# Graph encoder on one core: a separate buffer for the last keys' adjacency, a new order of VectorE's work at part ends, and three late projections emptied by ScalarE

## The chip, the core and the metric

The kernel runs on one core of a Trainium2 chip. The core has five engines, each with an instruction list of its own that it runs strictly in order: TensorE (PE; its weight loads are shown as PEld), VectorE (DVE), ScalarE (ACT), GpSimd (POOL) and SyncE (SP). Here POOL and SP do little but issue DMA transfers. Engines wait for each other through semaphores. Matrix products go into PSUM, which the kernel divides into eight banks of 128 partitions by 512 fp32 numbers; everything else lies in SBUF or in DRAM. The metric is the device time of one execution in microseconds (us).

## The reference

Four graph layers run on the same 2708 nodes of 512 features. The change touches the first part of the first layer, called the encoder here:

```python
Xh = X.reshape(n, H, D).transpose(1, 0, 2)            # H = 4 heads, D = 128
Xw = jnp.einsum('hnd,hde->hne', Xh, W)
f1 = jnp.einsum('hnd,hd->hn', Xw, V[:, 0, :, 0])
f2 = jnp.einsum('hnd,hd->hn', Xw, V[:, 1, :, 0])
sig = jax.nn.sigmoid(f1[:, :, None] + f2[:, None, :])
local_att = _masked_softmax(local_pattern[None] * sig, lmask)
...
Xa = jnp.einsum('hij,hjd->hid', att, Xw)
...
Xn = _batchnorm(Xc, enc_bn_gamma, enc_bn_beta)
emb = _mlp_block(Xn, enc_mlp_W, ...)
```

So for every head there is a 2708 x 2708 table: a sigmoid of a sum of one number per row and one per column, times the 0/1 adjacency, a softmax over the connected nodes, and a product with the projected features. Both masks are the same adjacency here, so one table serves both. The decoder, two more attention layers and a mean layer follow; the change leaves them alone.

## The kernel before

**Tiling.** The table is worked on transposed, keys on partitions. The 2708 keys are 22 blocks (`NT`): 21 of 128 and a last one of 20, "the last keys". The columns (the nodes that receive) are two halves of 1354 (`HW`). The four heads are taken two at a time (`HP`). A *part* is one half with one pair of heads, in the order (half 0, heads 0 and 1), (half 0, heads 2 and 3), (half 1, heads 0 and 1), (half 1, heads 2 and 3). A part has 22 *steps*, one for each key block, 88 steps in all. The last keys come at place 11 of a part; their 20 rows are spread over four groups of partitions, so that their tile is only 384 columns wide (`FEW`).

**One step.** ScalarE forms the sigmoid as a tanh, one 128x1354 instruction for each head (L383). VectorE forms the softmax argument for both heads at once, 128x2708 (L378): tanh plus a constant, times the masked adjacency. ScalarE takes the exponential of it (L515). PE multiplies it with the projected values: for each head, 11 matmuls for 11 blocks of nodes (L548, two records each in the trace). A value block has 129 columns, the last of them ones, so the row sums of the softmax come out beside the product. Three node blocks share a PSUM bank; a head fills four banks (`po`), two heads all eight. They accumulate over the 22 steps of the part.

**The adjacency.** A step's adjacency tile `a` comes on SP's queue (L480) into one of four buffers (677 KB a load). In the first pair of heads of each half it comes raw and VectorE makes the mask from it in two instructions (L443 compares with zero, L444 adds a large negative number), and POOL stores the masked tile in DRAM (L448) for the second pair of heads, which loads it back. For the last keys the four buffers serve as well: small strip loads on SP (L430, L432) fill one of them. Five blocks of the second half are fetched and masked ahead, during the second part (`fetch_early`).

**Order.** A framework puts the instructions of each engine in order when the program is built; the engine then runs that list as it is. `tc.issue_after(x)`, here `behind(x)`, forces an instruction behind another one. Buffers of a pool are reused in turn: an instruction that writes a reused buffer waits until all readers of the earlier content are through, DMA stores among them. The encoder's loop (L560 to L605) works on step *k*: it opens the tanhs of step *k*, issues the exponential of *k*-1, the argument of *k* (`form`), and PE's products of step *k*-2 (`FRONT` = 2), then the mask of step *k*+2.

**Start.** `project` computes the projected values on PE block by block (`values_of`): a 128x512 copy out of PSUM (L317), by ScalarE or VectorE, and a halving of f2 by VectorE (L321, 128x4). The first 17 blocks are done at once. The other five are left for `rest`, which is called after the argument of step 1 and is pinned behind it. There ScalarE copies two of the five, VectorE three; two chunks of f1 follow, and the two small instructions `bm1` and `less` (L343, L344) end it. Then the first mask of the loop runs.

**Part ends.** When PE has finished the last step of a part, `keep` (L759) empties the eight banks: for each head a memset of a column of `rc` (L769) and for each of its groups the largest of sum and a tiny number (L781), the reciprocal (L782), and the product of the values with it (L783, 128x384 for a full bank). `keep` is called behind the newest argument. Then `turn` transposes the rows back on PE (L802), three banks' worth for a head, all in banks of the second head; VectorE or ScalarE copies each to `ft` (L823). In the same bank as a head's third transposed piece lies the transposed `rc` (L810), which VectorE copies to `sm` (L812) and POOL stores to `rs_d` in two DMAs (L814, L818). Statistics of `ft` follow (L825). At part ends `pending` is 2 for a step and 1 for the next, and the exponential of step *k*-1 is then issued behind ScalarE's copies of the second head. The products of later steps into the second head's banks wait for these copies. The last of the four parts has no step behind it: its turns are interleaved with weight transposes (`seam`).

**Pools.** The wide tiles `t`, `rows` among them, have five buffers; `a` has four; `sm` has the default of its pool, two.

Of the kernel before, what the change touches and what calls it, by code (L numbers as in the profile page):

```python
# [8 lines left out]
F32 = mybir.dt.float32  # L9
# [3 lines left out]
AF = mybir.ActivationFunctionType  # L13
ALU = mybir.AluOpType
# [3 lines left out]
P = 128  # L18
# [3 lines left out]
TINY = 1e-30  # L22
# [7 lines left out]
def gnn_stack_kernel(  # L30
# [158 lines left out]
    with ExitStack() as l0:  # L189
# [45 lines left out]
        def project(att, psum):  # L235
# [66 lines left out]

            def values_of(jt, scalar):
                j0, n = BLOCKS[jt]
                pxw = psum.tile([P, H // HP, BANK], F32, tag=f"po{jt % HB}", name="pxw")
                pv = pxw[:, :, : HP * (P + 2)].rearrange("p a (k e) -> p a k e", k=HP)
                for h in range(H):
                    nc.tensor.matmul(
                        pv[:n, h // HP, h % HP, :],
                        xT_sb[:, h, j0 : j0 + n],  # L310
                        w0x[:, h, :],
                        start=True,
                        stop=True,
                    )

                copy = nc.scalar.copy if scalar else nc.vector.tensor_copy
                copy(  # L317
                    xw[:n, jt, :, :P].rearrange("p (a k) d -> p a k d", a=H // HP, k=HP),
                    pv[:n, :, :, :P],
                )  # L320
                nc.vector.tensor_scalar(  # L321
                    f2h[:n, jt, :].rearrange("p (a k) -> p a k", k=HP),
                    pv[:n, :, :, P + 1],
                    0.5,
                    None,
                    ALU.mult,
                )
            AT_ONCE = NT - 5
# [3 lines left out]
            def rest(step):  # L332

                with tc.issue_after(step.ins):
                    for jt in range(AT_ONCE, NT):
                        values_of(jt, jt < AT_ONCE + 2)
# [7 lines left out]
                    return nc.vector.tensor_scalar(  # L344
                        less, prm_sb[:, MB_ENC, :], 1.0, None, ALU.subtract
                    )

# [47 lines left out]
        def encoder_pass(values, att, banks, finish, f1b, blocks, spread, rest):  # L395

            FRONT, LEAD = 2, 2
            tanh, args, exps, tiles, loads, fetched, brought = ([] for _ in range(7))
# [65 lines left out]
            def bring(k):  # L464
# [6 lines left out]
                if k < len(blocks):  # L471
                    a = blocks[k]
                else:
                    a = att.tile([P, HW], F32, tag="a", name="a", bufs=4)
                    if n < P:
                        load_strips(a, src, hf)
                    else:
                        with behind(*[spread] if k < len(blocks) + 2 else []):
                            loads.append(
                                nc.sync.dma_start(a[:n, :w], src[j0 : j0 + n, h0 : h0 + w])  # L480
                            )
# [45 lines left out]
            def form(k, *more):  # L527

                *_, rows, width = rows_of(k)
                t, a = tiles[k]  # L530
                with behind(*args[-1:], *more):
                    args.append(arguments(t[:rows], a, rows, width))

# [26 lines left out]
            for k in range(len(STEPS) + FRONT):  # L560
# [4 lines left out]
                if pending != 1 and 0 < k <= len(STEPS):  # L565
                    exponentials(k - 1)
                if inside and not pending:
                    form(k)
                    if k == 1:
                        args.append(rest(args[1]))  # L570
                        po = banks()
                if k >= FRONT:
                    part, place = STEPS[k - FRONT]
# [162 lines left out]
        with (  # L736
# [20 lines left out]
            def keep(hf, p, po, later):  # L757
# [9 lines left out]
                for k in range(HP):  # L767
                    rc = att.tile([P, NB], F32, tag="rc", name="rc", bufs=4)
                    nc.vector.memset(rc[:, NB - 1 :], 1.0)  # L769
                    rows = all_rows[:, k]  # L770
                    groups = []
                    for b in range(HB + 1):
                        own = list(range(b * PER, min(NB, (b + 1) * PER)))
                        whole = [r for r in own if NODES[hf][r][1] == P]
                        groups += [(b, g) for g in (whole, [r for r in own if r not in whole]) if g]
                    for b, g in groups:
                        m = NODES[hf][g[0]][1]
                        src = po[k][b][:m, g[0] % PER * DR : (g[-1] % PER + 1) * DR]
                        src = src.rearrange("p (r e) -> p r e", e=DR)
                        own = rc[:m, g[0] : g[-1] + 1]  # L780
                        nc.vector.tensor_scalar(own, src[:, :, P], TINY, None, ALU.max)  # L781
                        nc.vector.reciprocal(own, own)  # L782
                        nc.vector.tensor_tensor(  # L783
                            rows[:m, g[0] : g[-1] + 1, :],
                            src[:, :, :P],
                            own.unsqueeze(2).to_broadcast([m, len(g), P]),
                            ALU.mult,
                        )
# [1488 lines left out]
```

## Time and profile before

| | |
|---|---|
| median of three runs | 3121.74 us (3119.06 to 3122.14) |
| the profiled execution, its own time | 3120.7 us |
| its span in the profile | 3118.8 us |
| encoder, first mask of the loop to PE's last product | 41.66 to 487.05 us |
| argument L378, in the encoder | x88, mean 2882 ns |
| tanh L383, in the encoder | x167 full-size, mean 1411 ns |
| exponential L515 | x88, mean 2377 ns |
| mask, L443 and L444, full-size | x37 each, mean 835 and 1510 ns |
| product by the reciprocal L783 | x40, mean 444 ns |
| copies of `ft` L823: ScalarE, VectorE | x15, mean 540 ns; x9, mean 613 ns |
| `sm` copy L812 | x8, mean 269 ns |

How to read the lines that follow. The page gives the busy time of an engine, its share of the span and the number of its instructions. A window line gives, for one stretch of time, its length, and the busy time of PE, PEld, DVE, ACT and POOL with the number of instructions, then the clock granted to PE as a share of full speed, the share of time that the DMA engines were busy, and GB/s. A wait line names an engine, the tile and source line that waited, what released it, then the total in us, how many times, and the longest. A timeline line gives start, duration, engine, source line, operation, out <- in with shapes; a wait that ended there stands in brackets. A DMA line gives size and us from issue to landing. Durations overlap a little at their ends: an instruction of 2.96 us on VectorE can be followed by the next start after 2.89 us.

### The profile page before, as it was taken

The page shows a single profiled execution, that of the slowest core. Times are in us where ns is not written, and L with a number is a line of the kernel's source. Part 1 is how long each engine was busy: PE and PEld are TensorE (multiplying, and loading weights), DVE is VectorE, ACT ScalarE, POOL GpSimd, SP SyncE. Part 2 cuts the span into 40 slices and gives each one's busy share as a digit, 9 for nine tenths or more (in the row PEclk, how much of TensorE's full clock was granted, in tenths as well). Part 3 has the DMA queues.
Part 4 walks back from the last instruction along what each step waited for, and adds up shares of the span by engine and source line. Part 5 has one row for each costly group of instructions (what it writes and reads, how often), then busy time and mean ns, then how long its engine had stood idle before and what let it go on. Part 6 is the DMA issues. An engine that isn't in the chain of part 4 may idle for free.

```text
span 3118.8 us, 39610 instructions
## 1 busy us (share of the span) xinstructions
PE 3070.6 (98%) x15144; PEld 2336.9 (75%) x15144; DVE 2025.3 (65%) x3804; ACT 1353.1 (43%) x1655; POOL 175.2 (6%) x301
## 2 busy tenths in 40 slices
PE   8999999999999999999999999999999999999999
PEld 7999996544444447875588887787778888888886
DVE  7988966785885783452366668677555555555565
ACT  7999998587767350001133334435211111111111
POOL 1111100000000000000111101000010000000000
PEclk9999999999999999999999999999999999999999
DMA  8987964266445315530254445566331111111110
GB/s 277 333 313 251 321 235 144 79 232 221 161 173 192 108 42 158 144 97 31 67 166 133 136 138 165 164 177 184 108 95 36 50 51 51 51 51 50 50 52 29
DMA packets 207228, 430.10 MB, mean 138 GB/s; under 512 B 22218, under 2 KB 137598, under 8 KB 201294
## 3 DMA queue, kind: packets, MB, share of 16 engines
q1 hardware_dynamic: 182774, 326.20, 34.0%
q0 software_dynamic: 24256, 101.35, 8.9%
q8 instruction: 119, 1.95, 0.3%
q14 instruction: 71, 0.58, 0.1%
q10 hardware_dynamic: 8, 0.02, 0.0%
HBM read 330.07 MB, written 95.87 MB: 137 GB/s over the span
## 4 chain that ended last, share of the span: by engine, by line
PE 79%; ACT 8%; DVE 8%; issue 3%; DMA 1%; SPq 0%; DVEq 0%; ACTq 0%; POOLq 0%
PE po L1728 21%; PE ps_s L1523 18%; PE po L650 9%; PE ps_nb L1326 7%; PE ps_wide L1376 5%; PE po L548 4%; ACT t L383 4%; ACT t L515 3%; DVE t L378 2%; PE ps_v L131 2%; PE ps_sup L1934 2%; PE ps_hid L131 2%; PE ps_dec L1093 2%; PE ps_mlp L964 1%; DVE a L444 1%
## 5 line engine op out<-in xcount | busy, mean ns | idle before, releaser
L378 DVE SCALAR_TENSOR_TENSOR t<-t,a 128x2708 f32<-128x2708 f32 (+1 forms) x152 | 443.8, 2922 | 166.1 <-ACT t L383 165.8
L548 PE MATMUL po<-xw,t 128*128 128x129 f32 (+2 forms) x3872 | 428.2, 277 | 11.8 <-DVE rc L781 4.9
L548 PEld LDWEIGHTS po<-xw,t 128*128 128x128 f32 (+2 forms) x3872 | 422.8, 189 | 16.4 <-issue 7.9
L383 ACT ACTIVATE t<-f1b,f2h 128x1354 f32<-128x1354 f32 x296 | 404.4, 1412 | 34.2 <-PE po L650 34.2
L1523 PE MATMUL ps_s<-q,hT 128*128 128x256 f32 (+1 forms) x1848 | 405.5, 372 | 0.0
L1728 PE MATMUL po<-sup,e 128*128 128x256 f32 (+1 forms) x1512 | 398.2, 384 | 5.6 <-DVE c L1809 2.8
L650 PE MATMUL po<-t,emb 128*128 128x452 f32 (+3 forms) x1056 | 399.1, 547 | 4.3 <-ACT t L635 4.2
L1523 PEld LDWEIGHTS ps_s<-q,hT 128*128 128x128 f32 x1848 | 339.5, 190 | 49.5 <-issue 5.1
L650 PEld LDWEIGHTS po<-t,emb 128*128 128x128 f32 (+1 forms) x1056 | 194.2, 191 | 202.1 <-issue 189.2
L1728 PEld LDWEIGHTS po<-sup,e 128*128 128x128 f32 (+1 forms) x1512 | 264.7, 185 | 59.6 <-issue 19.8
L1728 PE MATMUL po<-held,T 128*128 128x256 f32 x1200 | 293.8, 380 | 0.0
L1728 PEld LDWEIGHTS po<-held,T 128*128 128x128 f32 x1200 | 227.0, 190 | 31.1 <-issue 0.9
L2129 DVE SCALAR_TENSOR_TENSOR e<-a_cols,ps_s 128x512 f32<-128x512 f32 (+1 forms) x121 | 79.6, 658 | 233.8 <-PE ps_s L1523 229.9
L1523 PE MATMUL ps_s<-hT 128*128 128x256 f32 (+2 forms) x968 | 213.8, 372 | 0.8 <-ACT sup L1941 0.7
L515 ACT ACTIVATE t<-t 128x2708 f32<-128x2708 f32 x88 | 209.2, 2377 | 8.8 <-DVE t L378 8.1
L1523 PEld LDWEIGHTS ps_s<-hT 128*128 128x128 f32 x968 | 175.1, 190 | 29.1 <-issue 3.9
L1326 PE MATMUL ps_nb<-hid_hi,at 128*128 128x512 f32 x484 | 185.6, 390 | 0.4 <-DVE at L1318 0.4
L635 ACT ACTIVATE t<-t 128x2708 f32<-128x2708 f32 x64 | 157.3, 2458 | 60.4 <-DVE t L378 60.2
L1326 PE MATMUL ps_nb<-hid_lo,at 128*128 128x512 f32 x462 | 180.0, 390 | 0.0
L2031 ACT ACTIVATE a_score<-a_score,neg_big 128x512 f32<-128x512 f32 (+3 forms) x131 | 88.4, 683 | 196.0 <-DMA a_score<-in_adjT_dram 98.9
L2121 ACT ACTIVATE q<-ps_wide,uq 128x256 f32<-128x256 f32 (+1 forms) x44 | 20.5, 465 | 335.7 <-PE ps_wide L1376 335.7
L1633 ACT ACTIVATE e<-e 128x512 f32<-128x512 f32 (+1 forms) x187 | 113.8, 615 | 118.2 <-DVE e L1632 117.9
(276 smaller groups left out, 3995.4 us busy)
## 6 DMA issues: line engine op xcount, KB each, us to landing
a<-adj_d SPq DMA_DIRECT2D x113, 677.0 KB
a_cols<-in_adjT_dram SPq DMA_DIRECT2D x200, 256.0 KB
kept<-t POOLq DMA_DIRECT2D x20, 1354.0 KB, 8.4
t<-kept SPq DMA_DIRECT2D x20, 1354.0 KB
raw<-in_adjT_dram SPq DMA_DIRECT2D x105, 256.0 KB
a<-in_adjT_dram SPq DMA_DIRECT2D x37, 677.0 KB
adj_d<-a POOLq DMA_DIRECT2D x37, 677.0 KB, 6.2
a_score<-in_adjT_dram SPq DMA_DIRECT2D x55, 256.0 KB
```

The source lines that it names most:

```text
L131: nc.tensor.matmul(ps[:n], xt[:, c, :n], w[:, c, :], start=(c == 0), stop=(c == C - 1))
L378: return nc.vector.scalar_tensor_tensor(t, t, GUARD, ab, ALU.add, ALU.mult)
L383: done = nc.scalar.activation(t[:, k, :], f1b[k][:n, :w], AF.Tanh, bias=f2h[:n, jt, h : h + 1], scale=0.5,)
L515: nc.scalar.activation(t, t, AF.Exp, scale=0.5)
L548: nc.tensor.matmul(po[k][b][:m, s * DR : (s + 1) * DR], t[own : own + n, k, i0 : i0 + m], values[own : own + n, jt, HP * p + k, :], start= ...
L635: nc.scalar.activation(t, t, AF.Exp, scale=0.5)
L650: nc.tensor.matmul(po[HB * k + q][:, :qw], values[r : r + n, jt, h * P : (h + 1) * P], t[r : r + n, k, q0 : q0 + qw], start=(place == 0), ...
L1326: nc.tensor.matmul(pos[it][:n], at, half[:, jt, :], start=(jt == 0 and k == 0), stop=(jt == NT - 1),)
L1376: nc.tensor.matmul(ps[:, :width], w(c, o), xt(c), start=(c == 0), stop=(c == C - 1),)
L1523: nc.tensor.matmul(ps[:, jb, i:w], keys[:, c, j : j + P], st["q"][:, c, i:], start=(c == 0), stop=(c == C - 1),)
L1633: return nc.scalar.activation(e, e, AF.Exp)
L1728: nc.tensor.matmul(po[bank][rows, half, :], lhsT, rhs, start=(k == 0 and half == 0) if first is None else first, stop=last, skip_group_che ...
```

## The change

There are three edits, all in the encoder.

*Late projections.* `rest` lets ScalarE copy three of the five late value blocks instead of two. For these three, ScalarE also does the halving of f2, as an activation `Copy` with scale 0.5. `rest` returns two instructions, VectorE's last one and ScalarE's last halving, and the exponential of step 0 is issued behind the latter.

*Last keys' buffer.* The masked or raw adjacency of the last keys gets a buffer of its own, `a_few` of 128x384 numbers, one buffer. It is loaded when the tile of place 4 of a part is brought, behind that tile's load, and taken at place 11. The four `a` buffers serve the 21 full blocks alone.

*Part ends.* In the step that ends a part, the argument is no longer formed ahead of `keep`. Instead `keep` gets it as a function: head 0's banks are emptied behind the argument before, each instruction of the head chained by `behind_this`; then the argument is issued behind head 0's last product; then head 1's banks behind that argument. In the last part, where no argument is left, the function hands its input back. The copies `sm` get one buffer instead of two.

```diff
@@ -300,6 +300,8 @@
                 load_columns(NCH - 1)
                 nc.sync.dma_start(prm_sb, prm)
 
+            AT_ONCE, taken = NT - 5, []
+
             def values_of(jt, scalar):
                 j0, n = BLOCKS[jt]
                 pxw = psum.tile([P, H // HP, BANK], F32, tag=f"po{jt % HB}", name="pxw")
@@ -318,14 +320,13 @@
                     xw[:n, jt, :, :P].rearrange("p (a k) d -> p a k d", a=H // HP, k=HP),
                     pv[:n, :, :, :P],
                 )
-                nc.vector.tensor_scalar(
-                    f2h[:n, jt, :].rearrange("p (a k) -> p a k", k=HP),
-                    pv[:n, :, :, P + 1],
-                    0.5,
-                    None,
-                    ALU.mult,
-                )
-            AT_ONCE = NT - 5
+                half = f2h[:n, jt, :].rearrange("p (a k) -> p a k", k=HP)
+                if scalar and jt >= AT_ONCE:
+                    taken.append(
+                        nc.scalar.activation(half, pv[:n, :, :, P + 1], AF.Copy, scale=0.5)
+                    )
+                else:
+                    nc.vector.tensor_scalar(half, pv[:n, :, :, P + 1], 0.5, None, ALU.mult)
             for jt in range(AT_ONCE):
                 values_of(jt, jt < 2 * NT // 3)
 
@@ -333,7 +334,7 @@
 
                 with tc.issue_after(step.ins):
                     for jt in range(AT_ONCE, NT):
-                        values_of(jt, jt < AT_ONCE + 2)
+                        values_of(jt, jt < AT_ONCE + 3)
                     h0, w = HSPAN[1]
                     for q, (q0, _) in enumerate(HCH[1]):
                         f1_rows(HB + q, later_rows[:, q0:], q == 0)
@@ -341,9 +342,10 @@
                     copies(xw[:, NT - 1].rearrange("p h e -> p (h e)"))
                     copies(f2h[:, NT - 1, :])
                     nc.vector.tensor_scalar(bm1, prm_sb[:, MB_DEC, :], 1.0, None, ALU.subtract)
-                    return nc.vector.tensor_scalar(
+                    last = nc.vector.tensor_scalar(
                         less, prm_sb[:, MB_ENC, :], 1.0, None, ALU.subtract
                     )
+                return last, taken[-1]
 
             return f1b, blocks, spread, rest
 
@@ -395,7 +397,7 @@
         def encoder_pass(values, att, banks, finish, f1b, blocks, spread, rest):
 
             FRONT, LEAD = 2, 2
-            tanh, args, exps, tiles, loads, fetched, brought = ([] for _ in range(7))
+            tanh, args, exps, tiles, loads, fetched, brought, few = ([] for _ in range(8))
             state = {"f1b": f1b}
 
             def rows_of(k):
@@ -470,15 +472,18 @@
                 src = adjT if prepare else adj_d
                 if k < len(blocks):
                     a = blocks[k]
+                elif n < P:
+                    a = few.pop()
                 else:
                     a = att.tile([P, HW], F32, tag="a", name="a", bufs=4)
-                    if n < P:
-                        load_strips(a, src, hf)
-                    else:
-                        with behind(*[spread] if k < len(blocks) + 2 else []):
-                            loads.append(
-                                nc.sync.dma_start(a[:n, :w], src[j0 : j0 + n, h0 : h0 + w])
-                            )
+                    with behind(*[spread] if k < len(blocks) + 2 else []):
+                        loads.append(
+                            nc.sync.dma_start(a[:n, :w], src[j0 : j0 + n, h0 : h0 + w])
+                        )
+                if STEPS[k][1] == 4:
+                    few.append(att.tile([P, FEW], F32, tag="a_few", name="a_few", bufs=1))
+                    with behind(loads[-1]):
+                        load_strips(few[0], src, hf)
                 last_load[:] = loads[-1:]
                 if prepare:
                     mask_block(a, hf, jt, rows, width, *args[-1:])
@@ -530,6 +535,7 @@
                 t, a = tiles[k]
                 with behind(*args[-1:], *more):
                     args.append(arguments(t[:rows], a, rows, width))
+                return args[-1]
 
             def node_sums(k, part, place, t):
 
@@ -562,15 +568,19 @@
                 copies_done = []
                 if inside:
                     open_step(k)
-                if pending != 1 and 0 < k <= len(STEPS):
-                    exponentials(k - 1)
-                if inside and not pending:
+                part, place = STEPS[max(0, k - FRONT)]
+                ends = k >= FRONT and place == NT - 1
+                if pending != 1 and k > 1:
+                    if k <= len(STEPS):
+                        exponentials(k - 1)
+                if inside and not pending and not ends:
                     form(k)
-                    if k == 1:
-                        args.append(rest(args[1]))
-                        po = banks()
+                if k == 1:
+                    done, scalar_done = rest(args[1])
+                    args.append(done)
+                    po = banks()
+                    exponentials(0, scalar_done)
                 if k >= FRONT:
-                    part, place = STEPS[k - FRONT]
                     t, _ = tiles[k - FRONT]
                     if place > 3 and later and part[1] > 0:
                         with behind(args[-1]):
@@ -585,9 +595,10 @@
                         for work in waiting:
                             work()
                         waiting = []
-                    if place == NT - 1:
-                        with behind(args[-1]):
-                            turns = finish(*part, po, later)
+                    if ends:
+                        turns = finish(
+                            *part, po, later, args[-1], lambda done: form(k, done) if inside else done
+                        )
                 if pending == 1:
                     exponentials(k - 1, *copies_done)
                 if inside and pending:
@@ -754,7 +765,7 @@
             mlp_w, last_po, last_later, last_turn = [], [], [], []
             ft = feat_tile("ft")
 
-            def keep(hf, p, po, later):
+            def keep(hf, p, po, later, behind_this, argument):
                 h0, w = HSPAN[hf]
                 if hf == 1 and p == 0:
                     with behind(*last_load):
@@ -766,27 +777,30 @@
                 all_rows = wide_tile(att, "rows").rearrange("p (k r d) -> p k r d", k=HP, d=P)
                 for k in range(HP):
                     rc = att.tile([P, NB], F32, tag="rc", name="rc", bufs=4)
-                    nc.vector.memset(rc[:, NB - 1 :], 1.0)
-                    rows = all_rows[:, k]
-                    groups = []
-                    for b in range(HB + 1):
-                        own = list(range(b * PER, min(NB, (b + 1) * PER)))
-                        whole = [r for r in own if NODES[hf][r][1] == P]
-                        groups += [(b, g) for g in (whole, [r for r in own if r not in whole]) if g]
...
+                    with behind(behind_this):
+                        nc.vector.memset(rc[:, NB - 1 :], 1.0)
+                        rows = all_rows[:, k]
+                        groups = []
+                        for b in range(HB + 1):
+                            own = list(range(b * PER, min(NB, (b + 1) * PER)))
+                            whole = [r for r in own if NODES[hf][r][1] == P]
+                            groups += [(b, g) for g in (whole, [r for r in own if r not in whole]) if g]
+                        for b, g in groups:
...
+                            behind_this = nc.vector.tensor_tensor(
+                                rows[:m, g[0] : g[-1] + 1, :],
+                                src[:, :, :P],
+                                own.unsqueeze(2).to_broadcast([m, len(g), P]),
+                                ALU.mult,
+                            )
                     kept.append((rows, rc))
+                    if k == 0:
+                        behind_this = argument(behind_this)
 
                 final = hf == NHALF - 1 and p + 1 == H // HP
 
@@ -808,7 +822,7 @@
                     cw = min(w, c0 + BANK) - c0
                     if b + 1 == TURNS:
                         done = nc.tensor.transpose(bank[:NB, BANK - P :], rc, ident)
-                        sm = att.tile([NB, P], F32, tag="sm", name="sm")
+                        sm = att.tile([NB, P], F32, tag="sm", name="sm", bufs=1)
                         nc.vector.tensor_copy(sm, bank[:NB, BANK - P :])
                         full = (NB - 1) * P
                         nc.gpsimd.dma_start(
```

More of the change, by code (lines that the diff above doesn't have):

```diff
@@ L776, in keep @@
[L776 to L788, printed above, removed]
+                    with behind(behind_this):
[7 more added lines that the diff above has]
+                        for b, g in groups:
+                            m = NODES[hf][g[0]][1]
+                            src = po[k][b][:m, g[0] % PER * DR : (g[-1] % PER + 1) * DR]
+                            src = src.rearrange("p (r e) -> p r e", e=DR)
+                            own = rc[:m, g[0] : g[-1] + 1]
+                            nc.vector.tensor_scalar(own, src[:, :, P], TINY, None, ALU.max)
+                            nc.vector.reciprocal(own, own)
+                            behind_this = nc.vector.tensor_tensor(
[4 more added lines that the diff above has]
+                            )
```

## The prediction

> **What bounds the kernel now.** I read the page's busy shares first, then busy time by stage, then the waits of each engine inside the encoder, then the timeline of one part end and of the late projections. The change touches the encoder alone (about 30 to 495 us of the 3118.8 us span).
>
> ```profile
> PE 3070.6 (98%) x15144; PEld 2336.9 (75%) x15144; DVE 2025.3 (65%) x3804; ACT 1353.1 (43%) x1655; POOL 175.2 (6%) x301
> ```
>
> The average names TensorE; by stage it is different. Busy time of PE, PEld, DVE and ACT in the four parts:
>
> ```profile
> 41.66:149.00 107.34, 102.97 (x929) 101.71 (x930) 104.27 (x63) 99.91 (x62) 23.48 (x37) 0.98 0.85 298
> 149.00:260.00 111.00, 109.24 (x1002) 108.04 (x1001) 89.63 (x79) 108.56 (x71) 11.88 (x22) 1.00 0.87 318
> 260.00:374.00 114.00, 111.40 (x1003) 110.11 (x1002) 101.39 (x86) 110.27 (x73) 15.86 (x29) 0.99 0.82 291
> 374.00:487.00 113.00, 110.96 (x1018) 110.00 (x1018) 81.24 (x103) 104.46 (x68) 8.17 (x15) 1.00 0.67 214
> ```
>
> In the first part VectorE sets the pace: mask (0.79 and 1.59 us from start to next start) and argument (2.89) make 5.27 us a step. In the other three ScalarE does: two tanhs (2.63) and one exponential (2.35) make 4.98 us. PE is nearly tied: 88 matmul records took 9.85 us at 87.31, 0.112 each, so a step's 44 take 4.93. PE trails: the last exponential runs from 477.77 to 480.23, PE ends at 487.05, 1.9 us more than one step's 4.93.
>
> Where these engines waited (total us, times, longest):
>
> ```profile
> DVE z L443 <- DMA a<-in_adjT_dram: 1.7, 1, 1.7
> ...
> PE po L548 <- DVE rc L781: 4.9, 3, 2.1
> ...
> ACT ft L823 <- PE po L802: 7.0, 5, 1.9
> ...
> ACT ft L823 <- DVE sm L812: 1.8, 2, 1.2
> ```
>
> The second and third line are what the change goes for. The fourth is the one to watch: ScalarE's last copy of a head, out of the bank that also holds the row sums, starts only after VectorE's `sm` copy of those sums. The first part end shows it:
>
> ```profile
> 158.18 2.72 ACT L383 ACTIVATE t<-f1b,f2h 128x1354 f32<-128x1354 f32 x2
> ...
> 160.36 0.27 DVE L812 COPY sm<-po 11x128 f32<-11x128 f32 x1
> ...
> 161.23 2.96 DVE L378 SCALAR_TENSOR_TENSOR t<-t,a 128x2708 f32<-128x2708 f32 x1
> ...
> 164.11 0.27 DVE L812 COPY sm<-po 11x128 f32<-11x128 f32 x1
> ...
> 164.31 2.96 DVE L378 SCALAR_TENSOR_TENSOR t<-t,a 128x2708 f32<-128x2708 f32 x1
> 164.42 0.43 ACT L823 COPY ft<-po 128x330 f32<-128x330 f32 x1 [0.58 <-DVE sm L812]
> ...
> 164.75 2.46 ACT L515 ACTIVATE t<-t 128x2708 f32<-128x2708 f32 x1
> ```
>
> One argument (161.23) stands between the two `sm` copies; the second argument (164.31) comes after both, and the next exponential starts at 164.75.
>
> **The change, part by part.**
>
> *Late projections (about -1.1).* VectorE's stretch behind the second argument runs from 37.91 to the first mask at 41.66, 3.75 us:
>
> ```profile
> 37.91 0.15 DVE L321 TENSOR_SCALAR f2h<-pxw 128x4 f32<-128x4 f32 x1
> 37.98 0.68 DVE L317 COPY xw<-pxw 128x512 f32<-128x512 f32 x1
> 38.57 0.22 DVE L321 TENSOR_SCALAR f2h<-pxw 128x4 f32<-128x4 f32 x2
> ```
>
> One 512-column copy (0.6 to the next start), three halvings (0.07 each) and a 0.24 us wait for PE go: 1.05 us. VectorE is the bound here, so it counts. ScalarE gains one copy (0.50) and three small activations, which the trace does not have in this shape; the nearest row is a 128x4 activation, 0.20 us. They stand ahead of the first exponential, which started at 35.13 and now starts about 36.2. Its cover is VectorE's stretch: the next argument, at 44.92, needs a tanh pair that then ends about 41.3. Bounds -0.8 (the wait returns elsewhere) to -1.3.
>
> *The last keys' own buffer (about -1.7).* The mask at 94.95 waited 1.7 us for a load issued at 87.46, when the store of its buffer's earlier tile had landed. With the last keys out of the four buffers, that load takes the buffer released one 5.27 us step earlier, which is more than the wait. Four small and three smaller strip loads move up on SP, past one 677 KB load there; that load's tile is needed some 10 us later. Bounds: 0, if the full DMA engines (share 0.99 to 1.0 at 85 to 100) only make another load late, and -1.7.
>
> *Banks ahead of the argument.* VectorE empties head 0's four banks as they fill, then forms the argument, then empties head 1. PE no longer waits for `rc` (4.9 us, three times), and ScalarE is not held up by the later argument itself: at the first end the argument would end near 155.8, and ScalarE is busy with tanhs until 155.83. But `sm` now has one buffer instead of two, and in the built program the second `sm` copy has moved: at the first and third end behind both arguments, at the second behind a mask's first half, an argument and a mask's second half. It also waits for the first head's two row-sum stores. Queued behind it: ScalarE's third copy, the exponential behind that copy, and six of PE's matmuls into that bank. Laying rows end to end:
>
> First end: PE's last step (ends 153.6, 4.93 long) fills head 0's first bank at 149.6. Emptying head 0 alone 3.3 (the final turn's: 483.01 to 486.3) gives 152.9; argument 2.89, 155.8; head 1 with three copies and `sm` 4.4 (the 5.25 of 155.98 to 161.23 less head 0's remnants), 160.2; two arguments 2.89 + 2.96, 166.1; `sm` 0.3, copy 0.36: exponential at 166.75 against 164.75, **+2.0**. The stores are no later: they landed at 165.6 and 165.8.
>
> Second end: start 260.0; head 0 3.3, argument 2.89, head 1 2.9, mask 0.8 + 1.6, `sm` and last rows 0.5, argument 2.89, mask 0.79, argument 2.96, mask 1.56, `sm` 0.3, copy 0.36: 280.8. Some 0.4 of the head's short instructions overlap, 280.4 against 277.8, **+2.6** (2.0 to 3.2).
>
> Third end: start 372.9, by the same terms VectorE reaches `sm` at 389.4 and the exponential starts at 390.0 against 388.22, +1.8. But here the stores were slow:
>
> ```profile
> kept<-t POOLq DMA_DIRECT2D x1, 1354.0 KB, 10.2
> ...
> rs_d<-sm POOLq DMA_DIRECT2D x1, 5.0 KB, 7.8
> ```
>
> The row-sum stores queue on POOL behind a kept tile. Issued at 383.3 and 383.8 and landing 7.7 later, 391.5, they put the exponential at 392.2, +4.0; landing when they did before, 392.9, +5.3. I take **+4.0**, between 1.8 and 5.3, by the row of the same two stores.
>
> A page puts such a store lower: the Trainium skill, DMA: Bandwidth & Descriptors, "Anatomy of one DMA", fits about 2.0 us plus bytes over 436 GB/s for one DMA alone. By it the third end would cost 1.8 and the sum be 2.2 less; the rows, 3.4 to 7.8 at the inner ends, decide.
>
> *Final turn (+0.4).* The `argument` call does nothing here; head 1 is emptied strictly after head 0, where the rows of 486.1 to 487.0 show them interleaved: 0.4. `sm` came 2.80 after `sm` and its stores, issued 491.68 and 492.19, took 1.6: no wait. If they took 4, as elsewhere, +2.4.
>
> PE idles longer at the ends, and its clock shows what that does:
>
> ```profile
> 100.00:105.00 5.00, 2.15 (x10) 2.15 (x11) 5.00 (x4) 4.66 (x3) 0.03 (x1) 0.74 1.03 411
> ```
>
> After 3.9 us idle the granted clock was 0.74, then 0.92 for 5 us each: 1.7 us of PE time. The last keys' step takes PE 1.42 us where ScalarE needs 3.4, so PE makes up 2.0 in each part, and I cost it at nothing; without that cover, 1.7 an end. The Trainium skill, TensorE: Matmul & The Clock Gate, "HAM oscillation", warns of PE gaps above about 3.4 us; taken at its halved rate the price would be as much again, 3.4 an end, under the same cover.
>
> **Sum.** -1.05 - 1.7 + 2.0 + 2.6 + 4.0 + 0.4 = **+6.2 us**. Behind the encoder nothing changes. The profiled execution took 3120.7 (span 3118.8 and 1.9 around it), 1.0 below the median; 3126.9 against it, 3127.9 against the median. I forecast **3128**.
>
> **Rivals.** *Stores land early* (2 in 10): `sm` is bound by VectorE alone at all ends: +4.0, 3125.7. For it: the first two ends. Against: the 7.8. *Stores bind everywhere, the mask still waits* (2 in 10): -1.05 + 2.8 + 2.6 + 5.3 + 2.4 = +12, 3133.8. For it: stores issued sooner sit behind the same kept tile, and DMA is full there. *Faster, since PE and not ScalarE sets the end* (0.7 in 10): the bound is PE's list, late exponentials fall into PE's 1.9 us of trail, and 4.9 of `rc` waits go: -1.05 - 1.7 - 4.9 = -7.7, 3114.0. It decides only while exponentials are late by less than 1.9; my first end alone uses that up. *The buffer brings no earlier load*: +7.9, within the main case.
>
> **How the numbers follow.** Main case 5.3 in 10, from +4 to +9, about 3 above and 2.3 below the bound. Against the median, 0.2% (6.2 us, about what a measurement of this kernel can tell from no change) is 3128.0, so the forecast stands on the bound. Slower: 3 + 2 = 5 in 10; same 2.3 + 2 + 0.2 = 4.5; faster 0.5. Range: low end +1, all gains whole and the ends at their low bounds (-1.3 - 1.7 + 1.4 + 2.0 + 1.8 + 0 = +2.2) less 1.2 for the spread of the runs, 3122.7; high end the second rival, 3133.8.
>
> **What would show it.** Right: the first mask near 40.6, no DMA wait of a mask in the first part, `rc` gone from PE's waits; ScalarE's waits for `sm` grown from 1.8 to some 12 to 16 us, 4 to 7 at each inner end, with two arguments between the `sm` copies. Wrong: a short wait of that copy, exponentials on time after the ends, or PE idle for `rc` still.

## The result and the profile after

The changed kernel took 3126.3 us in the median of 12 runs (3122.04 to 3130.19), the kernel before 3119.5 in 12 runs. The ratio is 1.0019, 95% interval 1.0011 to 1.0027: slower by about 6 us. The profiled execution took 3126.66, with a span of 3124.6 against 3118.8.

Every one of the 88 exponentials has a start time in ScalarE's timeline, before and after, so the change can be read as a ladder: how much earlier or later the same exponential starts. It is flat within each part and steps at the places that the edits touch.

| exponential of step | before | after | difference | step of the ladder |
|---|---|---|---|---|
| 4 (behind the late projections) | 58.47 | 57.56 | -0.91 | -0.91 |
| 12 (behind the last keys of part 1) | 100.34 | 97.76 | -2.58 | -1.67 |
| 22 (ahead of the first end) | 150.85 | 148.27 | -2.58 | 0 |
| 24 (behind it) | 164.75 | 166.83 | +2.08 | **+4.66** |
| 44, 46 (around the second end) | 261.13, 277.82 | 263.23, 281.86 | +2.10, +4.04 | **+1.94** |
| 66, 68 (around the third end) | 374.20, 388.22 | 378.24, 393.84 | +4.04, +5.62 | **+1.58** |
| 87 (the last) | 477.77 | 483.40 | +5.63 | 0 |

Behind the encoder another 0.2 is added: the first matmul into `ps_m` starts at 500.51 instead of 494.70, +5.81, which is the whole of the span's difference.

The timelines of the changed kernel where the two gains come from. ScalarE's halving of f2 (L326) is new, and the first mask starts at 40.74 instead of 41.66; the mask that had waited 1.7 us for its load starts at 92.37 with no wait in brackets:

```profile
37.45 0.18 ACT L326 ACTIVATE f2h<-pxw 128x4 f32<-128x4 f32 x1
37.52 2.46 ACT L520 ACTIVATE t<-t 128x2708 f32<-128x2708 f32 x1
...
40.74 0.85 DVE L445 TENSOR_SCALAR z<-a 128x1354 bf16<-128x1354 f32 x1
...
92.37 0.87 DVE L445 TENSOR_SCALAR z<-a 128x1354 bf16<-128x1354 f32 x1
```

What the engines of the changed kernel wait for in the encoder (total us, times, longest):

```profile
DVE sm L826 <- DMA rs_d<-sm: 2.9, 1, 2.9
...
ACT ft L837 <- DVE sm L826: 15.9, 3, 6.5
...
PE po L554 <- ACT ft L837: 7.5, 3, 3.5
```

The 4.9 us for which PE's products waited for `rc` (L793 now) are gone, as the change intends. In their place PE waits 7.5 for ScalarE's copies where it had waited 0.9, and ScalarE waits 15.9 for `sm` where it had waited 1.8. The first part end shows both causes:

```profile
157.46 5.84 DVE L380 SCALAR_TENSOR_TENSOR t<-t,a 128x2708 f32<-128x2708 f32 x2
...
158.94 1.07 ACT L837 COPY ft<-po 128x512 f32<-128x512 f32 x2 [0.62 <-PE po L816]
...
166.19 0.28 DVE L826 COPY sm<-po 11x128 f32<-11x128 f32 x1 [2.88 <-DMA rs_d<-sm]
166.50 0.44 ACT L837 COPY ft<-po 128x330 f32<-128x330 f32 x1 [6.49 <-DVE sm L826]
...
166.83 2.46 ACT L520 ACTIVATE t<-t 128x2708 f32<-128x2708 f32 x1
```

Two arguments (157.46, x2) now stand ahead of the second `sm` copy, where one did. When they are done, at 163.3, VectorE waits another 2.88 us until the first head's row sums have left the one `sm` buffer. ScalarE has copied the rest of the head by 160.0 and stands idle for 6.49 us.

### The profile page after: what moved, and what is told of

It reads as the page before. It is cut to its first block, busy times and chain, and to the rows that moved or that the text cites. A ratio compares the mean times of both kernels' runs of the same rounds, so it can differ in the third digit from the quotient of the medians.

```text
span 3124.6 us, 39587 instructions
## 1 busy us (share of the span) xinstructions
PE 3074.1 (98%) x15144; PEld 2335.7 (75%) x15144; DVE 2026.0 (65%) x3800; ACT 1354.1 (43%) x1659; POOL 176.3 (6%) x301
## 4 chain that ended last, share of the span: by engine, by line
PE 81%; DVE 7%; ACT 6%; issue 3%; DMA 2%; POOL 0%; SPq 0%; DVEq 0%; POOLq 0%; ACTq 0%
PE po L1742 22%; PE ps_s L1537 19%; PE po L661 9%; PE ps_nb L1340 7%; PE po L554 5%; PE ps_wide L1390 5%; ACT t L385 3%; PE ps_sup L1948 2%; PE ps_v L131 2%; PE ps_hid L131 2%; DVE t L380 2%; ACT t L520 2%; PE ps_dec L1107 2%; PE ps_mlp L978 1%; PE ps_e L1670 1%
## 5 line engine op out<-in xcount | busy, mean ns | idle before, releaser
L380 DVE SCALAR_TENSOR_TENSOR t<-t,a 128x2708 f32<-128x2708 f32 x148 | 439.8, 2975 | 169.3 <-ACT t L385 169.1
```

Of the source, the lines that this page charges most:

```text
L380: return nc.vector.scalar_tensor_tensor(t, t, GUARD, ab, ALU.add, ALU.mult)
```

## The experiments

Theory A: the time is lost to the single `sm` buffer, in two ways: the copy stands one argument later on VectorE's list, and it waits for the first head's stores. Theory B: it is lost to emptying head 0 ahead of the argument, since the argument and all behind it come later. The last columns of this table are the steps of the ladder in each kernel, always against the kernel before (exponentials 22 to 24, 44 to 46, 66 to 68), and then the last exponential.

| kernel | median, before beside it | ratio, 95% interval | end 1 | end 2 | end 3 | last |
|---|---|---|---|---|---|---|
| changed | 3126.3, 3119.5 | 1.0019 [1.0011, 1.0027] | +4.66 | +1.94 | +1.58 | +5.63 |
| no_ends | 3116.38, 3119.54 | 0.9992 [0.9983, 1.0] | +0.11 | -0.01 | +0.12 | -2.51 |
| two_sums | 3111.86, 3119.54 | 0.9978 [0.9969, 0.9987] | -0.28 | -2.32 | -1.20 | -6.04 |
| before_one_sum | 3130.14, 3119.54 | 1.0036 [1.0023, 1.0049] | +2.95 | +2.65 | +3.31 | +9.03 |
| order_back | 3122.61, 3119.54 | 1.0014 [1.0005, 1.0023] | +7.57 | -0.40 | +1.38 | +6.12 |
| late_copy_two_sums | 3123.18, 3119.61 | 1.0011 [1.0002, 1.0021] | +1.81 | +2.06 | +2.13 | +2.53 |
| kept_behind_sums | 3117.12, 3119.61 | 0.9994 [0.9984, 1.0003] | +0.56 | -0.05 | -1.30 | -1.19 |
| sums_by_scalar | 3109.99, 3119.61 | 0.9974 [0.9963, 0.9985] | -1.11 | -3.67 | -1.64 | -7.88 |

**The two gains without the part ends.**

```diff
-                if inside and not pending and not ends:
+                if inside and not pending:
...
-                        turns = finish(
-                            *part, po, later, args[-1], lambda done: form(k, done) if inside else done
-                        )
+                        with behind(args[-1]):
+                            turns = finish(*part, po, later)
```

`keep` is that of the kernel before, and the two `sm` copies lie in one tile, as in the next experiment.

> The late projections and the last keys' buffer stay; at the part ends the argument comes ahead of both heads' banks again, as in the kernel before, and the two row-sum copies `sm` have a place each. Both theories: every exponential from step 12 on starts 2.58 us earlier than in the kernel before (0.91 from the projections, 1.67 from the buffer), the three ends add nothing, and the time is 2.6 us below the kernel before, some 3116.9. If PE's own list set the end of the encoder, the time would not follow the exponentials and the gain would be below 2.

It took 3116.38, and the last exponential comes 2.51 us earlier. The projections and the buffer are worth what they seemed, the time follows the exponentials, and so the rest of the change costs about 8 us by the ladder (5.63 and 2.51), 10 by the medians.

**A place for each `sm` copy.**

```diff
+                sums2 = att.tile([Q + NB, P], F32, tag="sm", name="sm", bufs=1)
...
-                        sm = att.tile([NB, P], F32, tag="sm", name="sm", bufs=1)
+                        sm = sums2[k * Q : k * Q + NB]
```

> The changed kernel, with a place for each of the two `sm` copies of a part in one tile of 43 partitions; the second copy then stands one argument earlier on VectorE. Theory A (the single `sm` buffer costs the time, by order and by store): against the changed kernel the exponential behind the part end starts 5.9 us earlier at the first end, 4.4 at the second, 2.9 at the third, 13 together; the time is 7.4 below the kernel before, some 3112. Theory B (emptying head 0 ahead of the argument costs the time): the exponentials stay within 1 us of the changed kernel's and the time near 3126. A third: PE's list becomes the bound, the exponentials come 13 us earlier and the time falls by less, to about 5 below the kernel before.

It took 3111.86. At the second and third end the exponential comes 4.3 and 2.8 us earlier than in the changed kernel. At the first it is 4.9 for an expected 5.9; PE was late there, of which the last section tells. VectorE's timeline at the first end has one argument between the copies again, and no wait for a store:

```profile
157.78 0.26 DVE L827 COPY sm<-po 11x128 f32<-11x128 f32 x1
...
158.58 2.96 DVE L380 SCALAR_TENSOR_TENSOR t<-t,a 128x2708 f32<-128x2708 f32 x1
161.56 0.28 DVE L827 COPY sm<-po 11x128 f32<-11x128 f32 x1
161.88 2.98 DVE L380 SCALAR_TENSOR_TENSOR t<-t,a 128x2708 f32<-128x2708 f32 x1
```

Theory B falls: with a place for each copy, the new order of the part ends is a gain. Against no_ends, which differs in this order alone, the last exponential comes 3.5 us earlier and the median is 4.5 lower. Nobody moved the copy by hand; with a free place for it, the framework puts it one argument earlier.

**One buffer in the kernel before.**

```diff
-                        sm = att.tile([NB, P], F32, tag="sm", name="sm")
+                        sm = att.tile([NB, P], F32, tag="sm", name="sm", bufs=1)
```

> The kernel before with one buffer for `sm` instead of two and nothing else changed. Theory A: the second `sm` copy moves behind one more argument at each end, and the exponential behind it starts 2.9 us later at the first end, 2.7 at the second, and 5.0 at the third, where the first head's stores land 7.8 us after issue: 10.6 together, some 3130. Theory B: no more than 1 us at any end, some 3120.

This one number makes the kernel before 10.6 us slower by the medians, 9.0 by the last exponential. That the medians differ by just the 10.6 that were expected is luck: the three ends come to 8.9. In its timeline the first end reads like that of the changed kernel, two arguments and then the copy:

```profile
161.34 5.85 DVE L378 SCALAR_TENSOR_TENSOR t<-t,a 128x2708 f32<-128x2708 f32 x2
167.16 0.28 DVE L812 COPY sm<-po 11x128 f32<-11x128 f32 x1
```

The first two ends came out as expected, the third at +3.31 for 5.0: the stores landed 6.0 after issue, not 7.8, and the copy waited only 0.5 for them.

**The order back, one buffer still.** The argument of the step behind an end is held behind the second `sm` copy:

```diff
-                    form(k, *copies_done if not scalar else [])
+                    form(k, *copies_done if not scalar else [], *sums_done if pending == 1 else [])
...
-                        nc.vector.tensor_copy(sm, bank[:NB, BANK - P :])
+                        sums_done[:] = [nc.vector.tensor_copy(sm, bank[:NB, BANK - P :])]
```

> The changed kernel with its one `sm` buffer; the argument of the step behind a part end is held behind the second `sm` copy, so that the copy stands one argument earlier, as in the kernel before. This parts the order from the wait for the stores. Theory A: at the first end the stores land at 166.0 as they did, and nothing is gained (0); at the second they land 5.0 after 273.6 and 2.3 us are gained; at the third they land 5.6 after 387.2 and 0.4 is gained; 2.7 together against the changed kernel, some 3123. Were the order the whole of it, the gains would be 5.9, 4.4 and 2.9, as with two places. Theory B: nothing at any end.

The order alone brings little, since the wait takes its place: VectorE's waits for the store grew from 2.9 us to 10.1 in three waits, 7.1 of it at the first end.

```profile
DVE sm L827 <- DMA rs_d<-sm: 10.1, 3, 7.1
```

The time, 3122.61, was close to what was expected, but its parts were not. The first end cost 7.57, 2.9 more than in the changed kernel where no difference was expected. The third gained 0.2, and the second 2.3 as expected. At the first end the stores were issued at 158.92 and 159.43, 1.7 later than in the changed kernel, since PE was late (see below), and landed 9.8 later, where they had taken 8.5.

**Two places, the copy late.** The mirror of it: the second copy is held behind the newest argument, so the order is that of the changed kernel and only the wait is gone. The argument is formed ahead of the second head's turns for that:

```diff
+                    if inside and pending == 1:
+                        form(k)
                     if turns:
...
-                if inside and pending:
+                if inside and pending > 1:
                     form(k, *copies_done if not scalar else [])
...
-                        nc.vector.tensor_copy(sm, bank[:NB, BANK - P :])
+                        with behind(*newest if k else []):
+                            nc.vector.tensor_copy(sm, bank[:NB, BANK - P :])
```

> The changed kernel with two places for `sm`, but with the second copy held behind the newest argument, so that it stands where the single buffer had put it: the order of the changed kernel without its wait for the stores. If order and wait add up as the traces say, the first end costs 1.8 us against the kernel before (4.66 less the 2.88 that the copy waited for the stores), the second 1.9 and the third 1.6 as in the changed kernel; with 2.6 gained ahead of the ends the time is 2.7 above the kernel before, some 3122. If the wait merely covered another delay, the first end stays at 4.7 and the time at 3125.

The first end cost 1.81, as expected: of its 4.66 us in the changed kernel, 1.8 are order and 2.9 the store. Order means here the whole new order of the end against the kernel before, the copy's later place less what emptying head 0 first brings. At the second end order is all of it (2.06 here, 1.94 there). The third came to 2.13 for 1.6; of this, 0.35 falls on the exponential of step 67, which starts ahead of the copy. The time, 3123.18, is 3.6 above the kernel before for an expected 2.7.

**The row sums ahead of the kept tile.** Which part of a store's time is the queue? On top of order_back, the 1354 KB store of a kept tile, which POOL issues just ahead of the first head's row sums at the first and third end, is held behind them:

```diff
+                    store = lambda: nc.gpsimd.dma_start(kept[:n, :, :w], t)
+                    held.append(store) if hold else store()
...
                         copies_done = [turns.pop(0)(scalar, after)]
+                        if held:
+                            with behind(*sums_done[1:]):
+                                held.pop()()
```

> One buffer and the order of order_back, and on POOL's queue the first head's two row-sum stores go ahead of the kept tile (1354 KB) that stood ahead of them at the first and third end. Theory Q (a store lands only with the tile ahead of it in its queue): the stores at the first and third end land some 2.6 us after issue, as the second head's did at 166.8 in the changed kernel with nothing ahead; the copy's waits of 7.1 and 2.6 us go, both ends come to 0.3 to 1.2 below the kernel before, the second stays at -0.5, and the time is some 5 below the kernel before, 3114.5. Theory L (the load on the DMA engines makes them slow): they land 5 or more after issue as before, the waits stay, and the time is that of order_back, 3122.6.

At the third end the stores landed 2.7 and 2.4 us after issue and the wait is gone, as theory Q says. But they were also issued 4.6 us sooner than in order_back, ahead of a run of 677 KB loads, so this end does not part the two theories.

At the first end they were issued 0.5 later than in order_back and took 4.5 and 4.2, for 9.8 and 9.7, with nothing ahead of them in their queue, and 1.67 of the 7.1 us of wait remained. So the tile ahead is the larger part there, and something is left that theory L would explain: three 677 KB loads were issued there between 157 and 166. An empty queue is not enough for a fast store either: in the changed kernel the second head's store at the third end, issued at 393.77 when everything of POOL's had landed, took 6.1 us, with the DMA engines busy for 0.99 of the next 3.2. That the loads are the reason was not tested.

The second end came to -0.05 for -0.5; the copy waited 0.69 us there for stores that stood behind a 677 KB one. The time, 3117.12, is 2.6 above what was expected; its profile also loses 2.4 us in a place that the edit does not touch, a mask in part 1 that waits for its load.

**ScalarE copies its own row sums.**

```diff
-                        nc.vector.tensor_copy(sm, bank[:NB, BANK - P :])
+                        (nc.scalar.copy if scalar and k else nc.vector.tensor_copy)(
+                            sm, bank[:NB, BANK - P :]
+                        )
```

> Two places for `sm`, and the second copy of a part end made by ScalarE, right ahead of its own third copy of `ft`, so that no VectorE instruction stands between the bank and ScalarE. Against two_sums, ScalarE no longer waits for VectorE at the third copy (0.8, 1.7 and 0.7 us there) and pays one small copy of about 0.25: the ends gain 0.3, 1.3 and 0.3, and the time is some 3110, 9 to 10 below the kernel before. If PE's list is the bound by then, the exponentials come earlier by that much but the time stays at 3112.

It took 3109.99, 9.6 us less than the kernel before and 16 less than the changed one, and is the fastest of all that were tried. ScalarE's timeline at the second end has no wait any more:

```profile
269.51 1.40 ACT L840 COPY ft<-po 128x330 f32<-128x330 f32 x3
270.94 0.26 ACT L827 COPY sm<-po 11x128 f32<-11x128 f32 x1
271.22 0.43 ACT L840 COPY ft<-po 128x330 f32<-128x330 f32 x1
271.55 2.47 ACT L520 ACTIVATE t<-t 128x2708 f32<-128x2708 f32 x1
```

Against two_sums the ends gain 0.83, 1.35 and 0.44 for an expected 0.3, 1.3 and 0.3. Its interval and that of two_sums overlap, so the last 2 us rest on the ladder (-7.88 against -6.04), not on the times.

## Why the prediction was right, point by point

The forecast was 3128, slower by 6.2 us against the profiled execution; the spans differ by 5.8, the medians by 6.8. The mechanism was the right one, but two terms of the sum were off by more than 2 us and cancelled each other: the first end by +2.66, the third by -2.42. That the sum came so near is luck; with one of the two put right it would have been 8.9 or 3.8.

- *Late projections*, -1.05: measured -0.91. The first mask was to start near 40.6 and starts at 40.74. ScalarE's side came out later than reckoned: the first exponential at 37.52, not 36.2, with three waits for PE (1.2 us together). VectorE's stretch covered it all the same. The term is known to some tenths at best: the six other kernels with the same start stand at -0.76 to -2.40 at this exponential, and before_one_sum, whose start is unchanged, at +0.25.
- *The last keys' buffer*, -1.7: measured -1.67. The size is that of the wait in one profile of the kernel before; in before_one_sum, with the old buffers, the same mask waited 1.11. The mask's wait for its load is gone from the first part of the changed kernel. That it is gone for good is more than the runs show: two_sums, late_copy_two_sums, kept_behind_sums and sums_by_scalar have a mask in part 1 that waits 0.6 to 2.4 us, about 118 to 121 us into the span.
- *First end*, +2.0: measured **+4.66**. VectorE's rows were summed rightly (4.66 less the 2.88 of wait is 1.8). The step that failed is the sentence "The stores are no later: they landed at 165.6 and 165.8". It compares landings of the kernel before with a copy at 166.1, a time that leaves out the 2.75 us the sum itself gains ahead of this end. VectorE was ready at 163.3; the stores were issued 3.7 us earlier than before, at 157.21 and 157.73, and landed at 165.7 and 166.1, no earlier.
- *Second end*, +2.6 (2.0 to 3.2): measured +1.94. The term that was too large is head 1 with its mask halves and row sums, 2.9 + 0.8 + 1.6 + 0.5 = 5.8; from 268.14 to 273.19 it took 5.05.
- *Third end*, +4.0 (1.8 to 5.3): measured **+1.58**. VectorE alone was put at +1.8, and +1.58 is near it. The 7.7 us for the stores did not come: issued at 387.18, they landed 5.6 later, before VectorE reached the copy.
- *Final turn*, +0.4: measured +0.2, and no wait for the store there.
- *PE at nothing*: right in this profile. The clock fell behind the first and second end (0.66 for 165 to 170, 0.77 for 280 to 285), and the ladder still does not move within a part, down to PE's last product, 5.63 later as the last exponential. In three kernels of the experiments it was not nothing; the last section has them, and there a fall of the clock cost either of the 1.7 and 3.4 us that the prediction set side by side.
- *What would show it*: ScalarE's waits for `sm` were to be 12 to 16 us and are 15.9, with 6.5, 5.9 and 3.5 at the ends for "4 to 7", the third a little below. PE's products no longer wait for `rc`; one transposition (L816) still does, 0.7 us.

Both misses are about when a store lands. The prediction took over the moment of landing at the first end, and the time from issue to landing at the third. Neither belongs to the place. In these traces the first head's row-sum store lands behind the kept tile (1354 KB) ahead of it in POOL's queue. The DMA lines at the first end in the kernel before, then in the changed kernel, and then in the changed kernel at the third end (KB, us to landing):

```profile
kept<-t POOLq DMA_DIRECT2D x1, 1354.0 KB, 6.5
...
rs_d<-sm POOLq DMA_DIRECT2D x1, 5.0 KB, 4.7
...
kept<-t POOLq DMA_DIRECT2D x1, 1354.0 KB, 9.3
...
rs_d<-sm POOLq DMA_DIRECT2D x1, 5.0 KB, 8.5
...
kept<-t POOLq DMA_DIRECT2D x1, 1354.0 KB, 6.6
...
rs_d<-sm POOLq DMA_DIRECT2D x1, 5.0 KB, 5.6
```

Issued at 155.99 and 157.21, tile and store landed at 165.3 and 165.7; at the third end, issued at 385.97 and 387.18, at 392.5 and 392.7. In the kernel before it was 165.0 and 165.6, 392.1 and 392.4; in order_back 168.3 and 168.7, 393.0 and 393.2. In these six cases (first and third end of three kernels) the row sums come 0.2 to 0.6 us after the tile, and the tile takes between 6.3 and 10.7. The first head's stores of no_ends, two_sums, before_one_sum, late_copy_two_sums and sums_by_scalar make ten more: none lands ahead of its tile, eight come 0.2 to 0.6 behind it, and two, at the third end of no_ends and two_sums, 2.0 and 2.3. Why a tile takes 6.3 us once and 10.7 another time was not tested. kept_behind_sums shows it from the other side at the first end: put ahead of the tile, the stores took 4.5 and 4.2.

The Trainium skill, DMA: Bandwidth & Descriptors, section "Queues, rings and completion order", says, of the queues on which SP and ScalarE issue, that each DMA engine takes the descriptors of a queue in order and that the signal of completion is held until every earlier write of that engine has landed, whatever its queue; the landings on POOL's queue agree. The page's fit, some 2.0 us, which the prediction had set beside its rows, is near the 2.7 and 2.4 us of kept_behind_sums at the third end and far from most others: with nothing of POOL's in flight, stores took between 1.6 us (order_back, issued at 169.82) and 6.1 (changed kernel, at 393.77).

Of the rivals, the first ("stores land early", +4.0) holds at the third end and the second ("stores bind everywhere") at the first. The third, that PE sets the end, does not hold: PE's last product of the encoder moves with the last exponential to 0.02 us in all of the kernels but sums_by_scalar, where it gains 7.70 for 7.88.

## What to carry to other kernels

A buffer count is part of the schedule: halving it can add a wait and can also move the writer in an engine's list, and either alone undid the gains here (late_copy_two_sums, order_back). Before a transfer's time is carried over to a new moment, look what stands ahead of it in its queue: a 5 KB store landed behind the 1354 KB one ahead of it in all 16 cases. Where times of an old trace are compared, shift them by what the change gains ahead of that place. Read a change along one repeated instruction, before and after: the ladder of differences gives each edit a price from a single profile, where the runs spread over 8 us. How exact it is, kernels with the same edit tell: ends that nothing touches came back to 0.12 us (no_ends), the start only to some tenths, and in one kernel to 1.5.

## What was not expected of the hardware

The same gap on PE does not always cost the same clock. At the last keys' step of part 1 PE waits 2.0 to 2.2 us for an exponential, in all seven kernels that have the new buffer. Windows of the changed kernel (third last column: the granted clock):

```profile
95.00:100.00 5.00, 3.03 (x58) 2.67 (x56) 5.00 (x3) 4.35 (x3) 2.69 (x5) 1.00 0.94 316
100.00:105.00 5.00, 4.72 (x42) 4.73 (x43) 4.96 (x4) 5.00 (x4) 0.73 (x1) 1.00 1.01 390
```

and of two_sums:

```profile
95.00:100.00 5.00, 2.95 (x57) 2.59 (x55) 5.00 (x3) 4.35 (x4) 2.30 (x4) 0.91 1.00 322
100.00:105.00 5.00, 5.00 (x24) 5.00 (x25) 4.97 (x4) 5.00 (x4) 0.73 (x1) 0.50 0.77 217
```

One kept the full clock, and so did kept_behind_sums; the other ran 5 us at half of it. no_ends, order_back and sums_by_scalar also fell to 0.50 there, late_copy_two_sums to 0.67. The Trainium skill, TensorE: Matmul & The Clock Gate, "HAM oscillation", puts the danger at gaps above some 3.4 us; a fall followed gaps of 2.0 to 2.2 here, in five of these seven profiles. What decides between them is not shown. What a fall costs comes in two sizes: in windows of 1 us the clock stands at 0.50 for some 6.8 us in four of these kernels and for 3.4 in late_copy_two_sums, as in the kernel before behind its gap of 3.9, so that 3.4 or 1.7 us of PE time are lost. The longer gap had the smaller price.

In the kernel before and in no_ends VectorE does not wait for PE when it empties the banks of part 1, though the clock fell in both. With head 0 emptied ahead of the argument, its first instruction there waits for PE. It waited 0.36 us where the clock had not fallen (the changed kernel and kept_behind_sums), and 0.84 in sums_by_scalar, 1.16 in two_sums and 1.91 in order_back, each of which had lost 3.4. On the way a mask waited for its load, 1.02 us in sums_by_scalar and 0.77 in two_sums; added to the wait for PE, this makes PE 1.5 to 1.6 us later in all three than where the clock held. The longest of these waits:

```profile
148.47 0.16 DVE L794 TENSOR_SCALAR rc<-po 128x3 f32<-128x3 f32 x1 [1.91 <-PE po L554]
```

The argument, the exponential of step 23 and, in order_back, the row-sum stores came later by as much: between exponentials 22 and 23 the ladder loses 0.40 us in sums_by_scalar, 0.72 in two_sums and 1.48 in order_back, and nothing in no_ends, where the clock fell to 0.50 too. In the 12 runs of the changed kernel the time goes with the mean clock that was granted, 3122.8 on average at 0.998 (2 runs), 3125.5 at 0.997 (5), 3127.0 at 0.996 (3) and 3129.4 at 0.995 (2). What share of that is this one place was not measured.
